# One early iteration fewer in a quad-pipelined four-layer modulated convolution

## The chip, the cores and the metric

The kernel runs on one core of one Trainium2 chip. Time is the device time of one execution in microseconds (us). The engines are TensorE (PE, with its weight loads as PEld), VectorE (DVE), ScalarE (ACT), GpSimd (POOL) and SyncE (SP, which here issues nearly all DMAs). Each engine works through its own instructions in the order in which the program lists them; semaphores hold an instruction until what it reads is written and what it overwrites is read.

## The reference

128 samples of 64 channels by 1024 positions go through four convolutions ("same", "upsample", "same", "downsample"), whose weights are modulated by a per-sample style and demodulated; the input is added at the end. Cut to one layer:

```
s = style @ mw.T + mb
weight = SCALE * w * s[:, None, :, None]
demod = lax.rsqrt(jnp.sum(weight * weight, axis=(2, 3)) + EPS)
weight = weight * demod[:, :, None, None]
out = conv(x, weight) + b[None, :, None]     # with a blur around the up- and downsampling
...
x = x + out                                  # after the four layers
```

Nothing nonlinear stands between the layers. The kernel therefore makes one filter of nine taps for each sample out of the four weights and both blurs, and applies it to the sample once; the few positions at either end of a row, where the padding enters, are computed apart.

## The kernel before

Two samples lie side by side on the 128 partitions, 64 channels each, and two such pairs make a **quad**; there are 32 quads (q = 0 to 31), and a sample's tables are columns of small tiles (index `[:, q, r]`).

**Making the filter of a quad** is a chain of small matmuls, each followed by an eviction with a per-sample scale:

- `scale3(q)`: ACT scales the last layer's weights by table tA into two tiles wd (line 361, "wd<-w3x,tA").
- `stage1(q)` or, with fewer matmuls, `stage1_a(q)` and `stage1_b(q)`: PE multiplies by the third layer into PSUM psS; ACT evicts to S with tB or tBn. `stage1_b` adds into the PSUM tile that ACT has read after `stage1_a`; DVE and POOL (line 446) complete S.
- `stage2(q)`: PE multiplies by E (second layer with the blurs) into psR; ACT evicts to R with tC. Where `share(q)` ran an iteration earlier, the shorter form `stage2_rest` is used, with the differences Ed that `tap_differences` makes once on POOL.
- `stage3(q, part)`, or with fewer matmuls `stage3_b(q)` and `stage3_a(q)`: PE multiplies by the first layer into psW or psA; ACT evicts to Wf with t0. The last matmuls of `stage3_b` read sums that `r_sums` makes, on POOL ("R<-R", line 589) and in the entry iteration on DVE.
- `combine_a`, `combine_b`: DVE makes H, the filter's combinations for a short-product scheme.

**Applying it**: `in_g01`, `in_g2`, `in3`, `in04` (DVE) and `in1`, `in2` (POOL, lines 727 and 732) form sums T and G of the input X; `conv0` to `conv4` (line 754) multiply them by Wf or H, 24 matmul instructions of 340 columns each; `sum1`, `sum2` (DVE) and `output` (ACT, line 831, tables tb and td) finish the three output planes, `store` sends them out.

**Order.** The program is a software pipeline written out by hand: iteration q builds the filters of q+1 to q+4 while it convolves q and q+1. Iterations 0 to 3 are `early_turn(q)`, from `FIRST = AHEAD + 1 = 4` on `turn_of(q)` runs, whose first iteration is the "entry" (its branches `if entry`), and the last three are written out. In `early_turn` the iteration `q == AHEAD` is "twice": it builds two quads, q+3 with `stage1` and q+4 with `stage1_a`, `stage1_b`; the iteration ahead of it issues two `scale3`. `late(q)` makes the stores go plane by plane (six DMAs instead of two) and leaves out the early form's load; `turn_of` loads the three planes of quad q+3 at its head. `sharing(q)` starts one iteration after the entry.

**Tables by groups of samples.** `PART` cuts the 128 samples into 0 to 15, 16 to 31 and the rest (`REST`, quads 8 to 31). The tables of the first two groups are made in the set-up and in iteration 0. Those of REST, and three small constants per group (`SMALL`: `small(q)` on PE, `small_rest(q)` on DVE), are spread over iterations 1 to 7:

- `EXTRA[(q, i)]`: at three places of an early iteration: behind `copy_m3` (0), behind the first part of `conv1` and the outputs (1), and just ahead of `scale3` (2).
- `TABLES[q]`: near the head of a `turn_of` iteration, behind `in2`; `SIDE[q]`: in its middle, behind `in_g2`; `LATE[q]`: at its end, behind `in3` and ahead of `in1` and `scale3`.

`var_root` is two ACT instructions (lines 246, 248), `var_newton` three DVE ones (256 to 258), `table_A` two on DVE (288), the other tables and the vectors (`vector_*`, 878 to 885) are POOL's.

Of the kernel before, what the change touches and what calls it, by code (L numbers as in the profile page):

```python
# [63 lines left out]
def kernel(  # L64
# [110 lines left out]
    def zeros_to_y(sets, n, start=True):  # L175
# [15 lines left out]
    sc, ssq, var, dm, nw = (  # L191
        const.tile([P, NL, B], F32, name=n) for n in ("sc", "ssq", "var", "dm", "nw")
    )
# [61 lines left out]
    def newton(v, y, n):  # L255
        nc_v.tensor_mul(n, y, v)
        nc_v.scalar_tensor_tensor(n, n, -0.5, y, op0=ALU.mult, op1=ALU.mult)
        nc_v.scalar_tensor_tensor(y, n, 1.5, y, op0=ALU.add, op1=ALU.mult)
# [6 lines left out]
    def var_newton(bs, ls=slice(0, NL)):  # L265

        newton(var[:, ls, bs], dm[:, ls, bs], nw[:, ls, bs])
# [7 lines left out]
    def table(eng, t, bs, upper, lower, src, mul):  # L275

        qs = slice(bs.start // 4, bs.stop // 4)
        for rows, sel in ((T, upper), (Bo, lower)):
            sel = sel if isinstance(sel, tuple) else (sel,)
            n = 2 // len(sel)  # L280
            for i, s in enumerate(sel):
                v = src.rearrange("c (q s) -> c q s", s=4)[rows, :, s]
                dst = t[rows, qs, n * i : n * (i + 1)]
                if isinstance(mul, float):
                    eng.tensor_scalar_mul(dst, v, mul)
                else:
                    m = mul.rearrange("c (q s) -> c q s", s=4)[rows, :, s]
                    eng.tensor_mul(dst, v, m)

    def table_A(bs, d):  # L290
        table(nc_v, tA, bs, slice(0, 4, 3), slice(1, 3), sc[:, 3, bs], d)


    def table_B(bs):
        table(nc_g, tB, bs, ALT, DOWN, sc[:, 2, bs], sc[:, 1, bs])

    def table_Bn(bs):
        qs = slice(bs.start // 4, bs.stop // 4)
        nc_g.tensor_scalar_mul(tBn[:, qs], tB[:, qs], -1.0)

    def table_0(bs):
        table(nc_g, t0, bs, ALT, ODD, sc[:, 0, bs], 1.0)


    def table_C(bs, eng=nc_g):
        table(eng, tC, bs, slice(0, 2), slice(2, 4), dm[:, 1, bs], dm[:, 0, bs])

    def table_3(bs):
        table(nc_g, t3, bs, ALT, ODD, dm[:, 3, bs], var[:, 3, bs])
        table(nc_g, td, bs, slice(0, 2), slice(2, 4), dm[:, 3, bs], 1.0)  # L310

    def table_b(bs):
        table(nc_g, tb, bs, slice(0, 2), slice(2, 4), oc[:, bs], 1.0)
# [63 lines left out]
    def scale3(q, engs=(nc_a, nc_a)):  # L377
        wd = []
        src = w3 if q < DIRECT else w3x
        n = src.shape[1]  # L380
        for j in range(2):
            t = wd_pool.tile([P, 5, C], F32, tag="wd", name=f"wd{q}_{j}")
            scaled_copy(engs[j], t[:, :n], src, tA[:, q, j : j + 1])
            wd.append(t)
        chain[q] = wd
# [68 lines left out]
    def tap_differences():  # L454

        d = Ed[:, :4].rearrange("c (a b) o -> c a b o", a=2)
        for b in range(2):
            nc_g.tensor_sub(d[:, :, b], E[:, 4 * b : 4 * b + 5 : 4], E[:, 2:7:4])
        nc_g.tensor_sub(Ed[:, 4:], E[:, 3:8:4], E[:, 5:6].to_broadcast([P, 2, C]))
# [249 lines left out]
    def in3(q, pairs=BOTH_PAIRS):  # L709
        if q < NQ:  # L710
            X, t = Xs[q % NX], t_tile(q, "T3")
            nc_v.tensor_sub(t[:, pairs, 0, :NJ], plane(X, 3, pairs), plane(X, 1, pairs))  # L712
# [6 lines left out]
    def in_g2(q, pairs=BOTH_PAIRS):  # L719
        if q < NQ:  # L720
            X, g = g_tile(q)
            sum_of(plane(g, 2, pairs), plane(X, 3, pairs), 0.5, plane(X, 2, pairs), ALU.subtract)
# [154 lines left out]
    def vector_a1(bs):  # L877
        nc_g.tensor_mul(a1[:, bs], sc[:, 2, bs], sc[:, 1, bs])

    def vector_Da(bs):  # L880
        nc_g.tensor_mul(Da[:, bs], sc[:, 3, bs], dm[:, 2, bs])

    def with_bias(dst, v, l, bs):
        n = bs.stop - bs.start
        nc_g.tensor_mul(dst[:, bs], v[:, bs], bb[:, l : l + 1].to_broadcast([P, n]))

    def vector_c0(bs):
        with_bias(c0f, dm[:, 1], 0, bs)

    def vector_b1(bs):  # L890
        with_bias(b1s, sc[:, 2], 1, bs)

    def vector_c2(bs):
        with_bias(c2f, sc[:, 3], 2, bs)
# [29 lines left out]
    def const_rest(l, bs, src):  # L924
        src = src[:, : bs.stop - bs.start]
        if l == 2:
            nc_v.tensor_mul(oc[:, bs], src, dm[:, 3, bs])
            nc_v.tensor_scalar(oc[:, bs], oc[:, bs], bb[:, 3:4], None, op0=ALU.add)
        else:
            add, f = ((b1s, 2.0), (c2f, 1.0))[l]  # L930
            nc_v.tensor_mul(cc[l][:, bs], src, (a1, Da)[l][:, bs])
            nc_v.scalar_tensor_tensor(
                cc[l][:, bs], add[:, bs], f, cc[l][:, bs], op0=ALU.mult, op1=ALU.add
            )
# [28 lines left out]
    def blurred(g, src, k1, k3, part):  # L963

        for b, f in list(enumerate((k1, k3, k3, k1)))[2 * part : 2 * part + 2]:
            dst = g[:, b : b + K, :]
            nc_v.scalar_tensor_tensor(dst, src, f, dst, op0=ALU.mult, op1=ALU.add)
# [11 lines left out]
    def setup1(part):  # L979
        blurred(g1, woi[1], 0.25, 0.75, part)  # L980
# [134 lines left out]
    PART = slice(0, 16), slice(16, 32), slice(32, B)  # L1115
# [97 lines left out]
    REST = PART[2]  # L1213
# [7 lines left out]
    def high(n):  # L1221
        return Y[:, 1, NB + 4 : NB + 4 + n]
# [19 lines left out]
    def small_rest(q):  # L1242
        l, bs = SMALL[q]
        const_rest(l, bs, high(bs.stop - bs.start))

    def layers(i, j):
        return REST, slice(i, j)
# [3 lines left out]
        (1, 1): lambda: (small_rest(1), tap_shares()),  # L1251
        (2, 1): lambda: (small_rest(2), var_root(REST, Y[:, 0])),
        (2, 2): lambda: (table_B(REST), table_Bn(REST), vector_a1(REST)),
        (3, 0): lambda: (var_newton(*layers(2, 3)), var_newton(*layers(0, 2))),
        (3, 1): lambda: (table_A(REST, dm[:, 2, REST]), small_rest(3)),
        (3, 2): lambda: (
            table_b(PART[1]),
            table_0(REST),
            vector_b1(REST),
            vector_c0(REST),  # L1260
        ),
    }


    TABLES = {
        4: lambda: (table_C(REST), vector_c2(REST), vector_Da(REST), tap_differences()),
        5: lambda: table_3(REST),
        6: zeros,
    }
    SIDE = {  # L1270
        4: lambda: var_newton(*layers(3, 4)),
        5: lambda: small_rest(4),
        6: lambda: small_rest(5),
# [18 lines left out]
        27: lambda: blur_side(1, 2),  # L1292
    }

    LATE = {13: lambda: setup1(1)}

    def extra(*at):
        EXTRA.get(at, lambda: None)()
# [1 line left out]
    def side(work, q):  # L1300
        work.get(q, lambda: None)()

    AHEAD = 3
    FIRST = AHEAD + 1

    def sharing(q):
# [2 lines left out]
    def late(q):  # L1309
        return AHEAD <= q < NQ - 2  # L1310

# [6 lines left out]
    def early_turn(q):  # L1318
        n, c, s = q + 1, q + 2, q + 3 + (q >= AHEAD)
        twice = q == AHEAD  # L1320
        if q == 1:
# [84 lines left out]
        scale3(s + 1)  # L1406
        if q == AHEAD - 1:
            scale3(s + 2)
# [4 lines left out]
    def turn_of(q):  # L1413
# [36 lines left out]
        in_g2(c)  # L1450
        side(SIDE, q)
        if q in SMALL:
# [24 lines left out]
        in3(c)  # L1477
        side(LATE, q)
        if s == NQ:
# [157 lines left out]
```

## Time and profile before

| | us |
|---|---|
| median of 3 runs | 477.73 (477.62 to 478.21) |
| the profiled execution | 478.26 |
| its span | 476.48 |
| PE busy in the span | 469.4 |
| DVE busy | 417.6 |
| ACT busy | 310.2 |
| POOL busy | 164.0 |

The span runs from the first to the last profiled instruction; the profiled execution's time holds 1.78 us more, which lie around it. Lines of the timeline give start in us, duration in us, engine, source line, operation, output<-inputs, and how many like instructions the row merges; in brackets stands the idle time before it and what ended it. Most helpers record from one source line, so an instruction is recognised by its tiles.

### The profile page before, as it was taken

How to read it: one execution, taken by the hardware profiler on the slowest of the kernel's cores; microseconds unless marked ns; L12 is line 12 of the kernel's file. 1: busy time of each engine (PE TensorE's matmuls, PEld its weight loads, DVE VectorE, ACT ScalarE, POOL GpSimd, SP SyncE). 2: the span in 40 equal slices, each digit the busy share in tenths (PEclk: the TensorE clock that was granted, in tenths of full speed). 3: DMA queues.
4: the chain of work that ended last, by engine and by line, in shares of the span. 5: the costliest groups of instructions: out<-in, count | busy, mean ns of one | idle time of the engine just before them, and what ended most of it. 6: DMA issues, size and time to landing. Idle time of an engine off the chain costs nothing.

```text
span 476.5 us, 26723 instructions
## 1 busy us (share of the span) xinstructions
PE 469.4 (99%) x11928; PEld 354.6 (74%) x11928; DVE 417.6 (88%) x691; ACT 310.2 (65%) x709; POOL 164.0 (34%) x197
## 2 busy tenths in 40 slices
PE   8999999999999999999999999999999999999996
PEld 7877797877677776677776677766987788768963
DVE  4799998879889998899979899979999999999895
ACT  5465757577766676766667666667666767766443
POOL 3434033564435442233432233422334432333200
PEclk9999999999999999999999999999999999999999
DMA  7215456535455554345543465533455554455125
GB/s 223 67 72 178 135 181 208 149 111 170 144 150 159 172 172 130 122 151 167 165 151 120 135 167 153 178 124 125 147 176 155 167 153 145 147 145 174 64 91 192
DMA packets 50514, 70.70 MB, mean 148 GB/s; under 512 B 5664, under 2 KB 47328, under 8 KB 50400
## 3 DMA queue, kind: packets, MB, share of 16 engines
q1 hardware_dynamic: 49808, 68.32, 46.1%
q8 instruction: 93, 1.52, 1.5%
q10 hardware_dynamic: 592, 0.69, 0.5%
q14 instruction: 21, 0.17, 0.1%
HBM read 35.36 MB, written 33.62 MB: 145 GB/s over the span
## 4 chain that ended last, share of the span: by engine, by line
PE 95%; DVE 3%; DMA 1%; issue 0%; ACT 0%; SPq 0%; ACTq 0%; DVEq 0%
PE psA L754 45%; PE Y L754 11%; PE psR L468 9%; PE psA L572 7%; PE psW L572 7%; PE psS L390 6%; PE psR L534 4%; PE psA L468 2%; PE Y L995 2%; PE Y L337 1%; DMA par_s<-in_params_s 1%; DVE H L663 1%; DVE G L663 0%; PE psM L205 0%; DVE Y L663 0%; DVE y L813 0%
## 5 line engine op out<-in xcount | busy, mean ns | idle before, releaser
L754 PE MATMUL psA<-T,H 64*64 64x340 f32 x2304 | 186.4, 447 | 0.3 <-DVE y L663 0.2
L754 PEld LDWEIGHTS psA<-T,H 64*64 64x64 f32 x2304 | 92.9, 133 | 45.5 <-issue 2.3
L663 DVE SCALAR_TENSOR_TENSOR G<-X 128x1376 f32<-128x1376 f32 (+2 forms) x65 | 78.1, 1207 | 0.3
L727 POOL TENSOR_TENSOR T<-G 128x684 f32<-128x684 f32 x28 | 46.5, 1661 | 73.8 <-DVE G L663 73.8
L446 POOL TENSOR_TENSOR S<-S 128x128 f32<-128x128 f32 x28 | 22.1, 789 | 141.6 <-ACT S L361 141.5
L361 ACT ACTIVATE R<-psR,tC 128x448 f32<-128x448 f32 x63 | 36.5, 630 | 44.7 <-PE psR L468 24.8
L754 PE MATMUL psA<-T,Wf 64*64 64x340 f32 x768 | 64.2, 446 | 0.0
L754 PE MATMUL Y<-T,Wf 64*64 64x340 f32 x768 | 62.8, 451 | 0.0
L663 DVE SCALAR_TENSOR_TENSOR Y<-m,psA 128x340 f32<-128x340 f32 x64 | 33.1, 516 | 27.9 <-PE psA L754 26.7
L361 ACT ACTIVATE psW<-psA 128x128 f32<-128x128 f32 x100 | 19.3, 269 | 49.0 <-PE psA L572 44.9
L741 DVE TENSOR_TENSOR T<-G 128x1368 f32<-128x1368 f32 (+1 forms) x33 | 50.7, 1540 | 0.0
L361 ACT ACTIVATE Wf<-psW,t 128x256 f32<-128x256 f32 (+2 forms) x76 | 32.7, 480 | 26.7 <-PE psW L572 26.4
L712 DVE TENSOR_TENSOR T<-X 128x684 f32<-128x684 f32 x32 | 48.3, 1509 | 0.0
L468 PE MATMUL psR<-S,E 64*64 64x64 f32 (+1 forms) x1472 | 46.9, 238 | 0.0
L732 POOL TENSOR_TENSOR T<-G 128x684 f32<-128x684 f32 x28 | 46.5, 1661 | 0.0
L390 PEld LDWEIGHTS psS<-wd,w2n 64*64 64x64 f32 x1120 | 34.7, 133 | 12.8
L468 PEld LDWEIGHTS psR<-S,E 64*64 64x64 f32 x1472 | 39.6, 134 | 4.9 <-ACT psR L491 0.2
L754 PEld LDWEIGHTS Y<-T,Wf 64*64 64x64 f32 x768 | 30.7, 132 | 16.7 <-DVE Y L663 0.6
L831 ACT ACTIVATE o<-psA,tb,td 128x340 f32<-128x340 f32 x63 | 37.0, 647 | 6.3 <-PE psA L754 6.3
L754 PEld LDWEIGHTS psA<-T,Wf 64*64 64x64 f32 x768 | 30.8, 133 | 13.4
L831 ACT ACTIVATE o<-Y,tb,td 128x340 f32<-128x340 f32 x63 | 36.6, 638 | 4.5 <-PE Y L754 2.7
L831 ACT ACTIVATE o<-y,tb,td 128x340 f32<-128x340 f32 x62 | 38.6, 679 | 0.6 <-DVE y L813 0.6
(164 smaller groups left out, 834.9 us busy)
## 6 DMA issues: line engine op xcount, KB each, us to landing
out<-o SPq DMA_DIRECT2D x167, 170.0 KB, 2.7
X<-in_x SPq DMA_DIRECT2D x150, 172.0 KB, 3.5
X<-in_x SPq DMA_DIRECT2D x14, 516.0 KB, 5.7
out<-o SPq DMA_DIRECT2D x6, 510.0 KB, 5.8
out<-o SPq DMA_DIRECT2D x2, 340.0 KB, 2.7
Xe<-in_x_ends SPq DMA_DIRECT2D x1, 512.0 KB, 6.6
out<-o ACTq DMA_DIRECT2D x3, 170.0 KB, 2.5
par<-in_params SPq DMA_DIRECT2D x2, 192.0 KB, 3.9
```

Of the source, the lines that this page charges most:

```text
L361: nc_a.activation(dst, src, AF.Copy, scale=f)
L390: nc.tensor.matmul(ps[r][cols, at * C : (at + n) * C], weight[rows], wd[c if r == 0 else 1 - c][rows, taps], start=first, stop=last, skip_ ...
L446: nc_g.tensor_add(t[:, :, 2], t[:, :, 2], t[:, :, 0])
L468: nc.tensor.matmul(dst[r][cols], weight[rows], st[c if r == 0 else 1 - c][rows, slots, :], start=False, stop=last, skip_group_check=True,)
L572: nc.tensor.matmul(dst[r][cols], weight[rows], t[rows, c, slots, :], start=first, stop=last, skip_group_check=True,)
L663: nc_v.scalar_tensor_tensor(out, x, f, y, op0=ALU.mult, op1=op)
L712: nc_v.tensor_sub(t[:, pairs, 0, :NJ], plane(X, 3, pairs), plane(X, 1, pairs))
L727: eng.tensor_add(t[:, :, 0, :NJ], plane(g, 2), plane(g, 1))
L732: eng.tensor_sub(t[:, :, 1, :NJ], plane(g, 2), plane(g, 1))
L741: nc_v.tensor_sub(t[:, pairs, :, :NJ], both(a, PL), both(b, 1))
L754: nc.tensor.matmul(ps[s][cols, :NB], w, Ts[q, tag][rows, c, i, g : g + NB], start=(g == 0 and m == 3), stop=(g == K - 1), skip_group_check ...
L831: nc_a.activation(dst, src, AF.Identity, bias=add, scale=d3)
```

## The change

`AHEAD` goes from 3 to 2: three early iterations (0 to 2) instead of four; iteration 2 is the "twice" one and iteration 3 the entry of `turn_of`. What stood in `EXTRA` for iteration 3 finds places in `TABLES`, `SIDE` and `LATE`.

```diff
         (2, 2): lambda: (table_B(REST), table_Bn(REST), vector_a1(REST)),
-        (3, 0): lambda: (var_newton(*layers(2, 3)), var_newton(*layers(0, 2))),
-        (3, 1): lambda: (table_A(REST, dm[:, 2, REST]), small_rest(3)),
-        (3, 2): lambda: (
-            table_b(PART[1]),
+    }
+
+
+    TABLES = {
+        3: tap_differences,
+        4: lambda: (
+            vector_c0(REST),
+            table_C(REST),
             table_0(REST),
             vector_b1(REST),
-            vector_c0(REST),
+            vector_c2(REST),
+            vector_Da(REST),
         ),
-    }
-
-
-    TABLES = {
-        4: lambda: (table_C(REST), vector_c2(REST), vector_Da(REST), tap_differences()),
         5: lambda: table_3(REST),
         6: zeros,
     }
     SIDE = {
+        3: lambda: (var_newton(*layers(2, 3)), var_newton(*layers(0, 2))),
         4: lambda: var_newton(*layers(3, 4)),
...
-    LATE = {13: lambda: setup1(1)}
+    LATE = {
+        3: lambda: (table_A(REST, dm[:, 2, REST]), small_rest(3), table_b(PART[1])),
+        13: lambda: setup1(1),
+    }
...
-    AHEAD = 3
+    AHEAD = 2
     FIRST = AHEAD + 1
```

## The prediction

> **What bounds the kernel now.** I read the page first: its busy shares and its chain of waits.
>
> ```profile
> PE 469.4 (99%) x11928; PEld 354.6 (74%) x11928; DVE 417.6 (88%) x691; ACT 310.2 (65%) x709; POOL 164.0 (34%) x197
> PE 95%; DVE 3%; DMA 1%; issue 0%; ACT 0%; SPq 0%; ACTq 0%; DVEq 0%
> ```
>
> TensorE (PE) is busy for 99% of the span, and the chain that ended last runs over it for 95%. So time is gained by giving PE less work, and any wait put into PE's order is paid in full, since nothing later is idle enough to win it back. Next the list of PE's waits, whole run (who waited for whom, total us, times, longest):
>
> ```profile
> PE Y L181 <- DVE eps L156: 1.4, 1, 1.4
> PE psM L205 <- issue: 0.5, 1, 0.5
> PE psA L754 <- DVE y L663: 0.2, 1, 0.2
> PE psA L754 <- DVE T L727: 0.2, 1, 0.2
> ```
>
> After the set-up PE has hardly waited at all; there is no stall for the change to remove. Then the sums by window. I cut the windows at the first matmul of stage2, which opens each iteration: rows for iterations 1 to 7 of the order as it is, columns busy us (instructions) of PE, PEld, DVE, ACT, POOL, clock, DMA share, GB/s.
>
> ```profile
> 44.63:58.92 14.29, 14.29 (x313) 11.01 (x305) 13.34 (x23) 8.82 (x18) 0.46 (x1) 1.00 0.57 186
> 58.92:73.90 14.98, 14.98 (x328) 13.11 (x328) 13.25 (x22) 9.31 (x20) 6.65 (x5) 1.00 0.58 182
> 73.90:89.30 15.40, 15.40 (x360) 12.30 (x356) 13.19 (x28) 10.94 (x23) 3.49 (x8) 1.00 0.43 150
> 89.30:101.92 12.62, 12.62 (x305) 9.42 (x298) 9.38 (x19) 7.13 (x18) 10.51 (x16) 1.00 0.40 117
> 101.92:116.50 14.58, 14.58 (x348) 11.04 (x347) 13.90 (x23) 10.97 (x26) 6.65 (x8) 1.00 0.59 187
> 116.50:130.52 14.02, 14.02 (x394) 10.16 (x391) 12.62 (x22) 9.79 (x24) 6.72 (x17) 1.00 0.51 153
> 130.52:144.51 13.99, 13.99 (x392) 10.15 (x390) 12.49 (x21) 9.75 (x24) 5.66 (x6) 1.00 0.51 154
> ```
>
> Iterations 1 to 3 are of the early form, 4 (12.62 us) is the entry, 5 the first regular one (its quad 7 is still built unshared), 6 and 7 regular with the shared taps. The granted clock is 1.00 throughout.
>
> **Term 1, PE's work.** Afterwards iteration 2 is the last early one and builds two quads (5 with stage1, 6 with stage1_a/b), 3 is the entry, 4 is regular with an unshared stage2 as 5 is now, and from 5 on all share. One early iteration is replaced by a regular one: one stage2 and one stage3 more take the shared form. The extra stage1 moves from iteration 3 to 2; its price is the time from its first matmul to the next conv1 matmul, 83.36 to 84.37, in these rows (start, us, engine, line):
>
> ```profile
> 83.36 1.18 PE L390 MATMUL psS<-wd,par 64*64 64x128 f32 x47
> 84.37 1.36 PE L754 MATMUL psA<-T,H 64*64 64x340 f32 x15
> ```
>
> That is 1.01. Now iterations 2 to 6 take 14.98 + 15.40 + 12.62 + 14.58 + 14.02 = 71.60. Afterwards: (14.98 + 1.01) + 12.53 + 14.58 + 14.02 + 14.02 = 71.14, where the entry is shorter by an estimated 0.09, since its constant's matmuls have 16 columns and not 96, and 14.02 stands for both iterations with a 96-column one. Term 1 is **-0.46 us**; from nothing (were the shared form no cheaper) to -0.6.
>
> **Term 2, the roots of the later samples in front of an eviction.** `var_root(REST)` stays at (2, 1), but iteration 2 now is the one that builds two quads. ScalarE's (ACT's) order becomes: evict stage1(5), output o<-y, the two root instructions, then evict stage1_a(6); stage1_b(6) adds into the same PSUM tile and cannot start before that eviction has read it. The rows: the same place in the present iteration 3, then what the roots cost in iteration 2.
>
> ```profile
> 84.62 0.94 ACT L361 ACTIVATE S<-psS,tB 128x320 f32<-128x320 f32 x2 [1.53 <-PE psS L390]
> 85.45 1.22 ACT L831 ACTIVATE o<-y,tb,td 128x340 f32<-128x340 f32 x2
> 86.95 0.84 ACT L361 ACTIVATE S<-psS,tBn 128x256 f32<-128x256 f32 x2 [0.27 <-PE psS L390]
> 87.93 0.44 PE L390 MATMUL psS<-wd,w2n 64*64 64x64 f32 x16
> ...
> 71.76 0.57 ACT L246 ACTIVATE dm<-Y,eps 128x384 f32<-128x384 f32 x1
> 72.69 1.17 ACT L831 ACTIVATE o<-psA,tb,td 128x340 f32<-128x340 f32 x2
> ```
>
> The eviction ends at 86.95 + 0.84 = 87.79 and PE goes on at 87.93: no slack there. Ahead of the eviction ACT idles 0.27. The roots take 72.69 - 71.76 = 0.93, so the eviction ends 0.93 - 0.27 = 0.66 later. I take **+0.6**, with the bounds 0 and 0.93. Behind it on ACT stand only o<-psA and one scale3 (iteration 2 loses the other scale3 pair to iteration 1); they are done before the next eviction of R.
>
> **Term 3, table_A directly ahead of the scale3 that reads it.** Now table_A(REST) is made at (3, 1) in the middle of iteration 3. Afterwards it is the last vector work of iteration 3, behind in3, and scale3(8), the next ACT instruction, reads it. ACT works in order, so stage2(6)'s eviction into R waits behind scale3(8), and PE's stage3_b(6) waits for R. The rows of the place it goes to (the end of the present entry and the start of 5), and of the pieces:
>
> ```profile
> 101.45 0.14 DVE L1454 MEMSET Y<- 128x96 f32 x1 [2.37 <-ACT o L831]
> 103.44 0.86 DVE L663 SCALAR_TENSOR_TENSOR y<-psA,m 128x680 f32<-128x680 f32 x1
> 104.21 1.85 DVE L712 TENSOR_TENSOR T<-X 128x684 f32<-128x684 f32 x1
> ...
> 82.47 0.86 DVE L712 TENSOR_TENSOR T<-X 128x684 f32<-128x684 f32 x1
> 85.53 0.42 DVE L288 TENSOR_TENSOR tA<-sc,dm 64x48 f32<-64x48 f32 x2
> 86.33 0.86 DVE L663 SCALAR_TENSOR_TENSOR y<-psA,m 128x680 f32<-128x680 f32 x1
> ...
> 103.38 1.04 ACT L361 ACTIVATE wd<-w3x,tA 128x320 f32<-128x320 f32 x2
> 104.65 1.16 ACT L361 ACTIVATE R<-psR,tC 128x448 f32<-128x448 f32 x2 [0.23 <-PE psR L534]
> ...
> 100.86 0.41 PE L390 MATMUL psS<-wd,w2n 64*64 64x64 f32 x16
> 106.14 1.03 PE L572 MATMUL psA<-R,w0s 64*64 64x192 f32 x22
> 107.40 0.44 PE L572 MATMUL psA<-R,par 64*64 64x128 f32 x5
> ...
> 103.67 1.67 POOL L727 TENSOR_TENSOR T<-G 128x684 f32<-128x684 f32 x1 [2.83 <-DVE G L663]
> 105.89 0.76 POOL L589 TENSOR_TENSOR R<-R 128x256 f32<-128x256 f32 x1 [0.55 <-ACT R L361]
> 91.50 0.93 POOL L285 TENSOR_SCALAR tb<-oc 64x8 f32<-64x8 f32 x2
> ```
>
> In the entry VectorE (DVE) sits idle 2.37 before its memset, until ACT's output of Y is done at 101.45; the entry keeps that order, so DVE can't be at in3 earlier than the present 104.21. In3 itself took 0.86 alone (82.47) and 1.85 here (104.21), while POOL's in1 ran (103.67 to 105.34). Afterwards POOL's in1 stands behind table_b, which waits for DVE's small_rest(3), so POOL is idle during in3 and I take 0.86. Then table_A ends at 104.21 + 0.86 + 0.42 = 105.49, scale3 at 106.53, R at 107.69, against PE's stage3_b at 106.14 now. Term 3 is **+1.55**; the bounds are 0 (table ready when ACT comes, as now) and 2.54 (in3 at 1.85).
>
> [...]
>
> **Term 4, POOL behind the same wait.** table_b(PART[1]) goes from (3, 2) to the same place, ahead of in1(5) and of r_sums(6), whose result the last eight matmuls of stage3_b read. small_rest ends 0.80 after table_A's start (85.53 to 86.33), thus at 105.87; table_b 0.93, in1 1.67, r_sums 0.76 end at 109.23. PE would ask for it at 107.69 + (107.40 - 106.14) = 108.95. Term 4 is **+0.3**, from 0 to 1.0 (POOL's spans are rough). in2(5) and the tables come later by the same amount, with the rest of the iteration as cover.
>
> **Steps costed at nothing.** The newton steps go to SIDE 3: six instructions, from the first row to the end of the last,
>
> ```profile
> 79.11 0.25 DVE L256 TENSOR_TENSOR nw<-dm,var 128x96 f32<-128x96 f32 x1
> 80.64 0.36 DVE L258 SCALAR_TENSOR_TENSOR dm<-nw,dm 128x192 f32<-128x192 f32 x1
> ```
>
> 1.89 us, where three stand now; the 2.37 idle before the memset hides the difference of about 0.9, and without that cover table_A would be as much later. tap_differences moves to TABLES 3, and vector_c0, table_0 and vector_b1 join TABLES 4. They come out of an entry in which POOL is busy 10.51 us into an iteration in which it is busy 6.65 of 14.58; were the whole difference of 3.86 theirs, POOL would still be idle for 4. Their first reader is the constant's matmul at the end of iteration 4; without cover the S addition of stage1_b(8) would be late, which is read an iteration on. The load of quad 6 leaves the middle of iteration 2 for the head of 3, and the stores of quad 2 become six instead of two, in SP's queue:
>
> ```profile
> 70.69 1.68 SPq L146 DMA_DIRECT2D X<-in_x  x2
> 89.29 3.30 SPq L146 DMA_DIRECT2D X<-in_x  x6
> ```
>
> as the second row has it for quad 7 now, an iteration ahead of the first reader; the issues take 3.30. If that cover were gone, in_g2 and with it in04 would wait for the landing, and PE about as long.
>
> **The sum.** -0.46 + 0.6 + 1.55 + 0.3 = +2.0. The profiled execution took 478.26 us, of which the span is 476.48; it would take 480.3. It lies 0.53 above the median of the three runs shown (477.73), so the forecast for the median is **479.7 us** (+0.42%). I call a difference of up to 0.2% (0.96 us) no change, about what a measurement of this kernel can tell.
>
> **The rivals.**
> *The waits never reach PE* (terms 2 to 4 nothing, or term 2 alone): 477.3 to 477.9, no change. It asks for table_A 1.55 sooner, by 105.49 - 1.55 = 103.94. For it: the 2.37 of idle DVE in the entry, if the memset did not wait there. Against it: the DVE instructions behind the memset need stage1_b, which ends on PE at 100.86 + 0.41 = 101.27, so that 0.18 could be won and table_A still come at 105.3.
> *Only scale3's wait*, the roots and r_sums hidden: 477.73 - 0.46 + 1.55 = 478.8, just slower. For it: POOL's spans are rough, and 0.66 of late eviction is small.
> *in3 is still beside POOL's work* (1.85): 1.0 more, 480.7. Against it POOL's place in the order.
> *PE gains more than its matmul time*, faster: the early iteration's removal would have to save over 0.96, so twice term 1, with all waits hidden, at 476.7 or less. Its place is iterations 2 to 6, its price the difference of 14.29 (early) and 13.99 (regular), 0.30, plus the 0.2 wait on y; it decides only if the unshared 14.58 also fell to 14.0. Against it: that iteration's stage2 stays unshared.
>
> **How the numbers follow.** Forecast 0.53, waits absent 0.15, scale3 alone 0.13, in3 blocked 0.13, faster 0.06. The forecast's own range is 479.0 to 480.4. The range, 477.5 to 481.2, leaves out the faster case, about half of the first rival and what lies above 481.2, where several terms are at their upper ends (some 0.05). Slower than 478.69: the forecast's 0.53, in3's 0.13 and some 0.09 of scale3 alone, 0.75; faster than 476.77: 0.06; within: 0.19, the waits' 0.15 and the 0.04 left.
>
> **What would show it.** Term 1: iteration windows of about 16 (plus its wait), 12.5, then 14.0 from iteration 5. Term 2: PE waiting at psS for S of ACT in iteration 2. Term 3: ACT's wd waiting about 2 us for tA, and PE's psA<-R waiting for ACT's R once, at the start of iteration 4. Term 4: the last psA<-R matmuls waiting for POOL's R. If ACT's wd finds tA ready, or if in3 takes 1.85 there, I am wrong by that.

## The result, and the profile after

The changed kernel is slower: 483.17 us, median of 5 runs (481.85 to 483.40), against 477.73 (477.62 to 478.61) before; ratio 1.0092, interval 1.007 to 1.0114 (the ratio of the two medians, 1.0114, is the upper end of that interval). The direction was forecast, the size was not: +2.0 us forecast, +5.4 measured, 2.0 above the upper end of the range.

From the page of the changed kernel the busy shares and the chain that ended last, and then rows of the list of PE's waits:

```profile
PE 472.1 (98%) x12008; PEld 346.5 (72%) x12008; DVE 420.5 (87%) x692; ACT 311.9 (65%) x715; POOL 165.9 (34%) x198
PE 93%; DVE 3%; issue 2%; POOL 1%; DMA 1%; ACT 0%; SPq 0%; ACTq 0%; DVEq 0%; POOLq 0%
...
PE Y L181 <- DVE eps L156: 1.4, 1, 1.4
PE psM L205 <- issue: 1.2, 1, 1.2
PE psA L572 <- ACT R L361: 0.5, 1, 0.5
PE psA L572 <- issue: 0.3, 1, 0.3
...
PE psA L754 <- issue: 0.2, 1, 0.2
```

The new waits are of two kinds: one for ACT's R, which the prediction named, and several "issue", in which PE waited for nothing that the profile shows. These figures are smaller than the loss: the row for R has 0.5, though 0.96 us lie between the starts of the instructions on either side of that wait. The other 0.44 is the duration that the profile gives the matmul before the wait, whose end is modelled. The iteration windows tell more; cut as before, iterations 2 to 6 of the changed kernel (PE busy first, then the other engines, clock, DMA):

```profile
59.20:76.04 16.84, 16.65 (x376) 14.50 (x376) 13.33 (x22) 11.34 (x25) 4.87 (x4) 1.00 0.55 171
76.04:88.59 12.55, 12.55 (x304) 10.03 (x296) 10.44 (x22) 7.15 (x19) 8.60 (x11) 1.00 0.41 117
88.59:105.32 16.73, 16.07 (x356) 12.04 (x351) 15.75 (x28) 10.29 (x25) 10.57 (x14) 1.00 0.54 164
105.32:120.31 14.99, 14.81 (x389) 10.19 (x389) 13.55 (x22) 10.78 (x26) 6.08 (x8) 1.00 0.50 145
120.31:134.72 14.41, 14.34 (x395) 10.28 (x392) 12.60 (x22) 9.79 (x24) 6.68 (x17) 1.00 0.48 149
```

They take 75.52 where the same five took 71.60: 3.9 of the 4.9 us by which the span grew (481.4 against 476.5); 0.3 more lie ahead of iteration 2 (59.20 against 58.92) and the rest behind iteration 6. The entry, at 12.55, is as forecast (12.53). Iterations 5 and 6 should have been 14.02 each; they are 14.99 and 14.41, though no other engine's instruction was moved in front of PE there.

**The forecast waits are there.** Iteration 2, ACT and PE around the roots:

```profile
71.77 1.23 ACT L831 ACTIVATE o<-y,tb,td 128x340 f32<-128x340 f32 x2
72.89 0.57 ACT L246 ACTIVATE dm<-Y,eps 128x384 f32<-128x384 f32 x1
73.82 0.84 ACT L361 ACTIVATE S<-psS,tBn 128x256 f32<-128x256 f32 x2
74.35 0.76 PE L390 MATMUL psS<-wd,w2n 64*64 64x64 f32 x14
74.94 0.22 PE L390 MATMUL psS<-wd,w2n 64*64 64x64 f32 x2
```

The eviction, 73.82 to 74.66, has no idle in front of it now, and PE's stage1_b is drawn out behind it, from 74.35 to its last two matmuls at 74.94. At the border of iterations 3 and 4:

```profile
90.99 0.86 DVE L712 TENSOR_TENSOR T<-X 128x684 f32<-128x684 f32 x1
91.77 0.41 DVE L288 TENSOR_TENSOR tA<-sc,dm 64x48 f32<-64x48 f32 x2
...
92.22 1.01 ACT L361 ACTIVATE wd<-w3x,tA 128x320 f32<-128x320 f32 x2 [1.90 <-DVE tA L288]
93.14 1.14 ACT L361 ACTIVATE R<-psR,tC 128x448 f32<-128x448 f32 x2
...
93.80 1.29 PE L572 MATMUL psA<-R,w0s 64*64 64x192 f32 x18 [0.52 <-ACT R L361]
...
92.75 0.54 POOL L285 TENSOR_SCALAR tb<-oc 64x8 f32<-64x8 f32 x2 [5.11 <-DVE oc L928]
93.36 1.64 POOL L727 TENSOR_TENSOR T<-G 128x684 f32<-128x684 f32 x1
94.96 0.73 POOL L589 TENSOR_TENSOR R<-R 128x256 f32<-128x256 f32 x1
```

Line by line this is the forecast chain: in3 at 0.86 while POOL is idle (5.11 us up to 92.75), table_A, then scale3 after 1.90 of idle ACT, R, and PE; POOL's r_sums ends at 95.69.

**What was not forecast** shows best at the weight loads of iteration 5: changed kernel first, then the same place of run a_phase (below), where a pause is missing.

```profile
107.46 0.14 PEld L754 LDWEIGHTS psA<-T,H 64*64 64x64 f32 x2
107.47 0.14 PEld L468 LDWEIGHTS psR<-S,E 64*64 64x64 f32 x2
108.37 1.05 PEld L754 LDWEIGHTS psA<-T,H 64*64 64x64 f32 x18 [0.76 <-issue]
```

```profile
106.76 0.14 PEld L468 LDWEIGHTS psR<-S,E 64*64 64x64 f32 x2
106.81 1.34 PEld L758 LDWEIGHTS psA<-T,H 64*64 64x64 f32 x20
```

In the middle of conv2, behind its first four matmuls, PE starts nothing for 0.6 us, and the trace shows nothing that it waits for. To see what these places share I numbered PE's instructions (loads, matmuls and semaphore instructions, in order of start) and looked up the number at each idle time of PE marked "issue" where more than 0.29 us lie between the start of the instruction before and the next one (that is the length given), in every profiled kernel of this study (the a_ and b_ kernels are the experiments below):

```
kernel           us into the span: length in ns, instruction number
before           14.10: 794, 449
changed          14.19: 1417, 449;  70.01: 346, 3009;  108.37: 621, 4801;  254.52: 562, 12737
a_tableA         13.78: 1236, 449;  70.08: 822, 3009;  107.94: 578, 4801;  150.12: 445, 7105
a_roots          13.37: 300, 449;   106.44: 640, 4801
a_phase          13.76: 697, 449;   194.64: 315, 9665
b_phase          13.80: 410, 449;   132.99: 329, 6337;  363.46: 502, 18881
a_late_phase     13.20: 972, 449;   192.44: 461, 9665
a_spread_phase   13.75: 1359, 449;  151.96: 683, 7361;  195.09: 300, 9665
a_all            104.55: 881, 4801
a_all_phase      191.60: 421, 9665; 392.57: 351, 20673
b_worst          14.45: 1951, 449
a_all_worst      13.38: 740, 449
```

All 26 numbers leave the remainder 193 when divided by 256 (449 = 256 + 193, 4801 = 18 x 256 + 193). The smaller pause of iteration 6 (122.63 us, 0.287) does too: 5569 = 21 x 256 + 193. So these pauses lie whole multiples of 256 instructions apart. I read them as borders of blocks of 256 instructions in PE's program, at some of which the next block isn't there yet; the numbers and the queue below are what this reading rests on, no row says it. The pause at 449 lies in the set-up, which is the same in all twelve kernels, and yet lasts from under 0.29 to 1.95: a border's place alone does not fix its price. The page's queue of instruction transfers fits, before and after:

```profile
q8 instruction: 93, 1.52, 1.5%
```

```profile
q8 instruction: 94, 1.54, 1.4%
```

One transfer of 16,384 bytes for each 256 of PE's 23,986 instructions before (93 for 93.7 times 256), 24,146 after (94 for 94.3). In the changed kernel 94 transfers stand against 94 borders crossed; I count each one for the border behind the one near which it starts. In the packets of this queue a block's transfer starts some 0.8 us (median; -1 to 3.5) after PE has crossed the border one block earlier. At the pauses named at 70.01, 108.37 and 254.52 PE goes on 2.3 to 2.4 us after the start of the transfer (67.64, 106.00 and 252.18), of which the transfer itself is about 1.0. In none of the twelve kernels does PE cross a border less than 2.19 us after the start of the transfer that belongs to it. An estimate from these figures: a block worked off in less than some 3.1 us (0.8 + 2.3) would end in a pause, as far as its transfer starts at the median.

### The profile page after: what moved, and what is told of

Its sections match the earlier page's. It is cut to its first block, busy times and chain, and to the rows that moved or that the text cites. A ratio compares the mean times of both kernels' runs of the same rounds, so it can differ in the third digit from the quotient of the medians.

```text
span 481.4 us, 26911 instructions
## 1 busy us (share of the span) xinstructions
PE 472.1 (98%) x12008; PEld 346.5 (72%) x12008; DVE 420.5 (87%) x692; ACT 311.9 (65%) x715; POOL 165.9 (34%) x198
## 4 chain that ended last, share of the span: by engine, by line
PE 93%; DVE 3%; issue 2%; POOL 1%; DMA 1%; ACT 0%; SPq 0%; ACTq 0%; DVEq 0%; POOLq 0%
PE psA L754 44%; PE Y L754 11%; PE psR L468 10%; PE psA L572 7%; PE psW L572 6%; PE psS L390 5%; PE psR L534 3%; PE psA L468 2%; PE Y L995 2%; DMA par_s<-in_params_s 1%; DVE H L663 1%; PE Y L337 1%; DVE G L663 0%; PE psM L205 0%; DVE Y L663 0%
## 5 line engine op out<-in xcount | busy, mean ns | idle before, releaser
L754 PEld LDWEIGHTS psA<-T,H 64*64 64x64 f32 x2304 | 89.4, 133 | 49.4 <-issue 2.3
L468 PE MATMUL psR<-S,E 64*64 64x64 f32 (+1 forms) x1536 | 49.5, 238 | 0.1
L468 PEld LDWEIGHTS psR<-S,E 64*64 64x64 f32 x1536 | 41.3, 134 | 5.6 <-ACT psR L491 0.2
L754 PEld LDWEIGHTS Y<-T,Wf 64*64 64x64 f32 x768 | 28.6, 132 | 18.7 <-DVE Y L663 0.6
L754 PEld LDWEIGHTS psA<-T,Wf 64*64 64x64 f32 x768 | 29.3, 133 | 15.1
```

Source lines behind the costliest of these rows:

```text
L468: nc.tensor.matmul(dst[r][cols], weight[rows], st[c if r == 0 else 1 - c][rows, slots, :], start=False, stop=last, skip_group_check=True,)
L754: nc.tensor.matmul(ps[s][cols, :NB], w, Ts[q, tag][rows, c, i, g : g + NB], start=(g == 0 and m == 3), stop=(g == K - 1), skip_group_check ...
```

## The experiments

Two theories. **W**: the loss is the waits of the prediction. **F**: besides them PE runs out of instructions, and more often than before, because the change puts 160 instructions more into PE's program (24,146 less 23,986), so that the block borders fall at other places of the iterations.

**a_tableA and a_roots** each take one wait away; PE's stream of instructions stays as the changed kernel has it.

The first:

```diff
     SIDE = {
-        3: lambda: (var_newton(*layers(2, 3)), var_newton(*layers(0, 2))),
+        3: lambda: (
+            var_newton(*layers(2, 3)),
+            table_A(REST, dm[:, 2, REST]),
+            var_newton(*layers(0, 2)),
+        ),
...
-        3: lambda: (table_A(REST, dm[:, 2, REST]), small_rest(3), table_b(PART[1])),
+        3: lambda: (small_rest(3), table_b(PART[1])),
```

The second:

```diff
-        (2, 1): lambda: (small_rest(2), var_root(REST, Y[:, 0])),
-        (2, 2): lambda: (table_B(REST), table_Bn(REST), vector_a1(REST)),
+        (2, 1): lambda: small_rest(2),
+        (2, 2): lambda: (var_root(REST, Y[:, 0]), table_B(REST), table_Bn(REST), vector_a1(REST)),
```

> The changed kernel with table_A(REST) moved from LATE 3 into SIDE 3, behind the newton step of layer 2; TensorE's stream of instructions is the same. Theory W (the waits of the prediction): ACT's wd no longer waits for tA, PE's wait for R at the start of iteration 4 goes, and the time falls by about 1.4 us, to about 481.8. Theory F (PE runs out of instructions where its stream comes in blocks of 256, and that is the larger part of the loss): the pauses of PE marked 'issue' stay, so that the time stays at least 3 us above the kernel before. Rival (the loss came from one chain of waits): the time falls by 3 us or more.

> The changed kernel with var_root(REST) moved from (2, 1) to (2, 2), behind the eviction of stage1_a. Theory W: PE's wait for S of ACT in iteration 2 goes, 0.5 to 0.6 us less, about 482.6. Theory F: all other losses stay.

a_tableA took 482.30 (6 runs, 481.07 to 485.86; ratio to before 1.0096, 1.0063 to 1.0129), a_roots 481.31 (5 runs, 480.74 to 483.51; 1.0072, 1.0047 to 1.0097). Taking table_A's wait away gained less than the 1.4 expected, and the list of a_tableA's PE waits from 85 to 105 us, which has this one row, says why.

```profile
PE psA L572 <- POOL R L589: 0.9, 1, 0.9
```

The wait for R of ACT is gone, and in its place PE waits 0.9 for R of POOL: POOL's in1 and r_sums still stand behind table_b and the end of DVE's work. The wait moved on to the next in line: iteration 4 lasted 16.27 us, 0.46 less than the 16.73 of the changed kernel. In a_roots PE's iteration 2 fell to 15.95 us, the same as in a_all_phase below. That its time fell by 1.9 and not by 0.5 can't be put down to the roots: the pause in iteration 2 (346 ns at 70.01 in the changed kernel) was missing in this profile too. Both kernels stay over 3 us above the one before and keep the pause at instruction 4801, as F has it.

**a_phase and b_phase** leave the order alone and move the block borders. The columns of some products of quad 0 are worked off in two halves: the same columns, and 16 PE instructions more for each group. a_phase halves six groups (96 instructions), so that with the change's 160 the borders are moved by 256, a whole block; b_phase halves ten groups of the kernel before (160 instructions). The set is that of a_phase.

```diff
+    SPLIT = {(0, 2, 1), (0, 1, 0), (0, 2, 0), (0, 1, 2), (0, 2, 2), (0, 1, 1)}
...
-                    nc.tensor.matmul(
-                        ps[s][cols, :NB],
+                    cuts = (0, NB // 2, NB) if (q, m, g) in SPLIT else (0, NB)
+                    for j, k in zip(cuts, cuts[1:]):
+                        nc.tensor.matmul(
+                            ps[s][cols, j:k],
...
-                        Ts[q, tag][rows, c, i, g : g + NB],
+                            Ts[q, tag][rows, c, i, g + j : g + k],
...
```

> The changed kernel with six groups of quad 0's conv1 and conv2 cut into two column halves each: the same columns, 96 PE instructions more, so that from there on the borders of the 256-instruction blocks fall at the same places of the iterations as in the kernel before. Theory F: the pauses marked 'issue' in iterations 5, 6 and 15 go or shrink, and the time falls by 1 to 2 us, to 481 to 482. Rival (the pauses hang on the DMA traffic's timing, not on where the borders fall): unchanged within 0.5 us of 483.2.

> The kernel before with ten groups of quad 0's products cut into halves: the same columns, 160 PE instructions more, so that the block borders fall where they do in the changed kernel. Theory F: pauses marked 'issue' appear in the regular iterations and the time rises by 1 to 2 us, to 478.7 to 479.7. Rival: unchanged, 477.7 within 0.5.

a_phase took 480.63 (5 runs, 480.31 to 481.17; 1.0051, 1.0031 to 1.0070): 2.5 below the changed kernel, for 96 instructions that add no columns; 1 to 2 were expected. b_phase took 479.10 (10 runs, 478.06 to 480.57) against 477.92 for before on the same chip; 1.0022, 1.0008 to 1.0037: 1.2 us slower, with pauses at 132.99 and 363.46. Both agree with F and not with their rivals, a_phase by more than F's own figure. The halved groups have a price too: the stretch that holds them lasts 25.80 us in a_phase and 25.81 in b_phase, against 25.52 in the kernel before (19.11 to 44.63), so some 0.3 of b_phase's 1.2 is theirs.

Where the time goes can be read from the traces. Behind the halved groups two such kernels have the same PE instructions, so that they can be laid side by side, number by number. From 50.63 us of a_phase to the end the changed kernel falls behind it by 2.51 us: 2.78 of it within 16 instructions of the changed kernel's own block borders, -0.25 at a_phase's, -0.02 everywhere else. From 48.88 us of the kernel before to the end b_phase falls behind it by 0.85: 1.74 at its own borders, -0.77 at the other's, -0.12 elsewhere. The loss sits at the borders.

Windows of a_phase, iterations 2 to 6:

```profile
58.85:75.35 16.50, 16.43 (x377) 14.31 (x377) 13.33 (x22) 11.34 (x25) 4.87 (x4) 1.00 0.54 173
75.35:87.89 12.54, 12.54 (x304) 10.03 (x296) 10.45 (x22) 7.14 (x19) 8.59 (x11) 1.00 0.40 117
87.89:104.61 16.72, 16.07 (x357) 12.04 (x351) 15.74 (x28) 10.28 (x25) 10.56 (x14) 1.00 0.52 164
104.61:118.76 14.15, 14.15 (x389) 10.67 (x389) 13.57 (x22) 10.76 (x26) 6.85 (x8) 1.00 0.51 155
118.76:132.77 14.01, 14.01 (x395) 10.22 (x391) 12.62 (x22) 9.77 (x24) 6.69 (x17) 1.00 0.50 153
```

73.92 in all, 2.32 above the 71.60 of before: with the borders out of the way, nearly the +2.0 of the forecast.

**a_late_phase and a_spread_phase** go on from a_phase: the first takes away both waits at the head of iteration 4, the second thins out POOL's tables. The first, with table_A in SIDE 3 as in a_tableA:

```diff
-        3: lambda: (table_A(REST, dm[:, 2, REST]), small_rest(3), table_b(PART[1])),
+        3: lambda: small_rest(3),
...
         4: lambda: (
+            table_b(PART[1]),
             vector_c0(REST),
```

The second:

```diff
-        3: tap_differences,
+        3: lambda: (tap_differences(), table_0(REST), vector_b1(REST), vector_c2(REST)),
...
             table_C(REST),
-            table_0(REST),
-            vector_b1(REST),
-            vector_c2(REST),
             vector_Da(REST),
```

> The kernel of run a_phase, with table_A(REST) in SIDE 3 and table_b(PART[1]) first in TABLES 4, so that neither ACT's scale3 nor POOL's in1 and r_sums wait for the end of iteration 3's vector work. Theory W + F: PE's waits for R of ACT and for R of POOL at the start of iteration 4 both go (terms 3 and 4), 1.5 to 1.9 us below a_phase's 480.6, about 478.9. Rival (the wait moves on to the next in the queue, as in run a_tableA): less than 0.7 us below.

> The kernel of run a_phase with table_0, vector_b1 and vector_c2 in TABLES 3 instead of TABLES 4. Theory: POOL's run of tables in iteration 4 holds up DVE by about 1 us and through it ACT's copy of the shared taps, so that PE comes 0.3 us late to stage2 of iteration 5; that goes: 0.2 to 0.4 us below a_phase. Rival: no difference, since scale3's wait in the same iteration covers it.

a_late_phase took 478.94 (11 runs, 477.82 to 480.15; 1.0013, 0.9995 to 1.0032), 1.7 below a_phase, as expected. Its iterations 4 and 5:

```profile
87.36:102.22 14.86, 14.86 (x357) 11.50 (x352) 14.60 (x26) 10.44 (x26) 10.65 (x14) 1.00 0.58 183
102.22:116.21 13.99, 13.99 (x392) 10.63 (x388) 13.39 (x22) 10.53 (x26) 6.83 (x8) 1.00 0.52 159
```

Iteration 4 fell from 16.72 to 14.86: terms 3 and 4 together are 1.86. a_spread_phase took 480.18 (11 runs, 479.79 to 480.98; 1.0045, 1.0027 to 1.0062), 0.45 below a_phase; the intervals overlap, so this effect isn't settled by the times. Its iterations 4 and 5 lasted 16.59 and 13.91 in the trace, 0.37 less than a_phase's together.

**a_all and a_all_phase** have all the moves (roots, table_A, table_b, tables), the first with the changed kernel's block borders, the second with those of the kernel before.

> The changed kernel with all moves (roots, table_A, table_b, the tables of TABLES 4), the blocks of PE's stream where the changed kernel has them. W + F: no PE wait for another engine is left in iterations 2 to 4, but the 'issue' pauses stay: 1.0 to 2.0 us above a_all_phase, 478.4 to 479.4. Rival (W alone): equal to a_all_phase.

> All moves and the block borders of the kernel before. W + F: only term 1 is left, 0.46 us below the kernel before: 477.2 to 477.7. Rival (something else in the new order costs time): above 478.2.

a_all took 480.25 (11 runs, 478.78 to 482.18; 1.0045, 1.0024 to 1.0066), a_all_phase 477.90 (12 runs, 477.63 to 479.19; 0.9994, 0.9978 to 1.0011). The two have the same work and the same order and differ by 96 instructions at the start; the difference is 2.35 us, a little more than the 2.0 allowed for. The trace of a_all is that of its fastest execution (478.78) and shows 1.0 of it in the span (477.0 against 476.0). Windows of a_all_phase, iterations 2 to 6:

```profile
58.31:74.26 15.95, 15.95 (x376) 14.13 (x376) 13.35 (x22) 10.59 (x23) 4.95 (x4) 1.00 0.57 180
74.26:86.77 12.51, 12.51 (x304) 9.35 (x297) 11.48 (x24) 8.03 (x21) 9.96 (x15) 1.00 0.40 116
86.77:101.46 14.69, 14.69 (x354) 11.34 (x350) 14.42 (x26) 10.61 (x26) 7.84 (x10) 1.00 0.59 181
101.46:115.47 14.01, 14.01 (x394) 10.13 (x391) 13.22 (x22) 10.36 (x25) 6.80 (x8) 1.00 0.55 162
115.47:129.63 14.16, 14.16 (x395) 12.63 (x391) 12.55 (x22) 9.71 (x24) 6.49 (x17) 1.00 0.49 150
```

The first four take 57.16, against 14.98 + 15.40 + 12.62 + 14.58 = 57.58 for the four of before: 0.42 less. All five, the windows that term 1 sums, take 71.32 against 71.60: 0.28 less. So the order with one early iteration fewer saves about what it should in these windows, once PE waits for no other engine there. In the time a saving of 0.1% is too little to be measured: a_all_phase is the best version of the new order and no better than the kernel before.

**b_worst and a_all_worst** were to show the size of F by putting the borders where PE works off 256 instructions fastest (128 instructions more in the kernel before, 224 in a_all).

> The kernel before, untouched but for eight groups of quad 0's products cut into halves: 128 PE instructions more, the same columns. Read from the trace of before, 256 PE instructions last 3.6 to 3.9 us at the shortest where its block borders fall now in iterations 6 to 9 and 20 to 28; with the borders 128 instructions on they would last 2.8 to 3.3. A block's transfer starts about 0.8 after the border and is of use 2.3 later, thus 3.1 in all. Theory F: a pause of some 0.2 to 0.5 in most of those 13 iterations, 2 to 5 us in all: 480 to 483. Rival (the pauses of the changed kernel were chance of the DMA traffic): 478 to 479, as b_phase.

> The changed kernel with all moves and 224 PE instructions more, so that its borders fall as in b_worst. Theory F: 2 to 5 us above a_all_phase's 477.9, the same as b_worst within 1 us. Rival: as a_all, 479 to 480.5.

b_worst took 479.36 (11 runs, 478.27 to 480.48; 1.0023, 1.0009 to 1.0038), a_all_worst 479.50 (11 runs, 478.65 to 481.33; 1.0027, 1.0010 to 1.0043). They agree with each other, and the kernel before loses 1.4 us to instructions that add no columns, some 0.3 of it for the halved groups; but 2 to 5 us were expected, and that failed. a_all_worst lies in the range of its rival (479 to 480.5), so by its time it doesn't tell the two apart, and b_worst lies between the ranges of both. The traces point to F in the main: laid beside the kernel before, b_worst falls behind by 1.05 us from 48.88 us on, 1.30 of it within 16 instructions of its own borders, -0.70 at the other's and 0.44 elsewhere. Beside a_all_phase, a_all_worst falls behind by 1.20 (1.43, -1.13 and 0.90), so here the borders are not all. The shortest blocks between these borders do last only 2.7 to 3.35 us in the two traces, but their transfers mostly start earlier, 0.2 before to 0.5 after the border. The start of a transfer is thus no constant 0.8 behind the border, and which borders are bad can't be read off from the block's time alone.

## Why the prediction was wrong, and where it was right

**Right** in mechanism and size, by runs of their own: term 1 as PE's work, -0.46 forecast, -0.42 over iterations 2 to 5 of a_all_phase and -0.28 with iteration 6. Term 2, +0.6 forecast: iteration 2 lasts 16.50 in a_phase and 15.95 with the roots moved, 0.55. Terms 3 and 4, 1.55 + 0.3 forecast: 1.86 for the two together; no run takes term 3 away and leaves POOL's wait as it was. The choice of in3 at 0.86, and not 1.85, was right: in3 found POOL idle and took 0.86 (90.99 of the changed kernel). What held it to 1.85 beside POOL's in1 was not shown. In the order of the changed kernel these waits cost what was forecast, and the rivals with fewer or longer waits for other engines are out.

**Wrong** was a step of term 1: "14.02 stands for both iterations", which took it that a stretch of the program lasts as long in a new place as in the old. The regular iterations were taken over with their times, those behind iteration 6 too, and these hold only for where the block borders fell. Moved by some 160 instructions, the same iterations 5 and 6 lasted 14.99 and 14.41; a_phase, with the borders put back, has 14.15 and 14.01, and lies at 480.63, inside the range. The missing part is the 2.5 us between the two: by theory F the supply of PE's instructions, a term that the sum doesn't have. In the traces 1.6 of it lie in iterations 2 to 6 (75.52 against 73.92). That a_phase is still 0.9 above the forecast is open in part; some 0.3 are its halved groups, and some 0.4, by one trace, the tables of the next paragraph. The sign of the missing term was on the quoted list: of the rows of PE's waits one was `PE psM L205 <- issue`, 0.5 us without any releaser, and the prediction passed over it as "after the set-up PE has hardly waited at all".

Also overlooked, and small: POOL's tables in iteration 4 were costed at nothing because POOL had idle time. ACT's copy of the shared taps, ahead of PE's stage2 of iteration 5, has this row in the changed kernel:

```profile
104.91 0.63 ACT L491 COPY psR<-psA 128x256 f32<-128x256 f32 x2 [1.07 <-DVE S L443]
```

It waited 1.07 for DVE's part of S, and DVE was busy for 15.75 of that iteration's 16.73 us, beside 10.57 of POOL. With the tables thinned out the two iterations lasted 0.37 less; that is one trace, and the times alone don't settle it.

**Open** is what sets the start of a block's transfer (-1 to 3.5 us after the border), and whether the spread of a kernel's times comes from it (a_all 478.78 to 482.18 in 11 runs, a_all_phase 477.63 to 479.19 in 12). Kernels with less DMA traffic beside the transfers were not tried.

## What to carry to other kernels

PE, busy for 99% of the span in the kernel before and 98% in the changed one, paused 26 times in 12 kernels for over 0.29 us without a releaser, each time at a block border, and 96 instructions without added columns took 2.5 us off the time (a_phase): a pause marked "issue" with no releaser is to be numbered by instruction before it is put down to anything else, and two versions whose instruction counts differ are to be compared with the count made equal. A move in an in-order queue is to be followed through to the second in line: taking table_A away uncovered POOL's r_sums and saved 0.46 of iteration 4, both together saved 1.86. And work given to an idle engine was not free here: the same in3 on DVE took 1.85 us beside POOL's in1 (104.21 of the kernel before) and 0.86 beside an idle POOL (90.99 of the changed kernel).

## What the runs showed of the hardware that was not expected

Every one of the 26 pauses of PE over 0.29 us without a releaser, in 12 kernels, fell on the same remainder (193) of the instruction number by 256. Shifting PE's stream by 96 to 160 instructions, with the same columns to multiply, moved the time by +1.2 us (b_phase), -2.5 (a_phase) and -2.35 (a_all to a_all_phase). At the three pauses named, PE goes on 2.3 to 2.4 us after the transfer of the block has started, though the 16 KB themselves take about 1.0; in 12 kernels no border is crossed sooner than 2.19 us after that start.
